# Four conv-like layers on one core: where an output product, a tile copy and the parameter load stand in their queues

## The chip, the cores and the metric

The kernel runs on one core of a Trainium2 chip. The metric is device time in microseconds (us) of the whole program, from the first to the last instruction; the median of several executions counts. A core has a matrix engine (TensorE, PE in the profile; its weight loads are PEld), a vector engine (VectorE, DVE), an activation engine (ScalarE, ACT), GpSimd (POOL) and a queue engine (SyncE, SP) that here only starts DMA transfers. Each engine works through its own instruction list; semaphores order them against each other. PSUM is the accumulator memory that TensorE writes.

## The reference, cut to what matters

Four images of 512 channels and 64 x 64 points go through four layers. Layer 0 is softmax attention over all 4096 points with 64 channels, layer 1 a convolution whose weights are mixed from eight experts by a router, layer 2 a linear attention, layer 3 two discounted running sums with a gate.

```python
# layer 0
t = einsum('oc,bchw->bohw', w_qkv, x)               # key, query, value: 64 channels each
scores = einsum('bdk,bdq->bkq', key_, query)         # 4096 x 4096 for each image
attn = softmax(scores, axis=1)                       # over the keys
out = einsum('bdk,bkq->bdq', value, attn)
x = scale * einsum('oc,bchw->bohw', w_out, out) + x
# layer 1
pooled = x.mean(axis=(2, 3)); rw = sigmoid(pooled @ router_w.T + router_b)
# ... three convolutions with W = sum over experts of rw * experts, batch norms g, b, m, v, relu
# layer 2
Q = softplus(Wq x + bq); K = softplus(Wk x + bk); V = Wv x + bv
KV = einsum('bmn,bcn->bmc', K, V)
x = x + gamma * einsum('bnm,bmc,bn->bcn', Q, KV, 1 / einsum('bnm,bm->bn', Q, K.sum(-1) + EPS))
# layer 3
# ... x + gamma * x_gate * sigmoid(discounted sums of x_scan along both axes)
```

## The kernel before

Everything is in float32. An image's points are worked on in four "pairs" of 2 x 512 points. Double PSUM banks come from one pool of three, which scores, output products and transposes share in turn; there are two single banks beside it.

```python
def pair_psum(name):
    return ps.tile([P, 2, NB], F32, tag="s", name=name, bufs=3)
def bank(name, shape=(P, NB)):
    return ps.tile(list(shape), F32, tag="acc", name=name)   # 2 buffers
```

The kernel starts with loads. `prm` holds all small parameters, 50 floats for each of 128 partitions; the first image's x comes in 16 pieces.

```python
for queue, k in ((nc.scalar, 0), (nc.sync, 2)):
    queue.dma_start(wqkv_sb[:, k:k + 2, :], wqkv_t[:, k:k + 2, :])
prm_sb = const.tile([P, NPRM], F32, tag="prm", name="prm_sb")
nc.scalar.dma_start(prm_sb, prm)
xs = [load_pair(0, pr) for pr in range(NPAIR)]     # b == 0: four pieces of 512 KB for each pair
# ... [cut]
for j, n, _, _, _, v in groups:                     # batch norm from the parameters
    nc.vector.tensor_scalar(bn_v[:, j:j + n], col(v, n), 1e-5, None, ALU.add)          # L155
nc.scalar.activation(bn_s, bn_v, AF.Sqrt)                                               # L156
nc.vector.reciprocal(bn_v, bn_s)                                                        # L157
# ... [cut: three products or differences for each group, L159 to L161]
```

The projections of the first image follow the steps of a list. A digit is a matrix product, `v0:1` a value product of pair 0 with channel piece 1, `seed` a copy by ScalarE (L317) that the product `2` accumulates upon, `t5` the difference of the two pairs (L257) that the product `5` reads.

```python
first = ("zero v0:0 1:0 v0:1 1:1 seed v0:2 2:0 v0:3 2:1 t5 5 c11 v1:0 v1:1 t6 ...")     # [cut]
```

In the attention, a step i computes scores of 128 keys with one pair of queries, their exponential goes to a ring of 12 buffers, VectorE adds it to the pair's sum, and later a product with the values reads it. A pair has 32 steps, a round 8 steps; an image has 16 rounds, numbered 0 to 15. Values lag scores, so a pair ends in rounds 4, 8 and 12, and the last one after the loop.

```python
def scores(i):
    pr, kt = divmod(i, NT)
    s = pair_psum(f"s_{b}_{i}")
    for h in range(2):
        nc.tensor.matmul(s[:, h, :], key[...], qry[...], start=True, stop=True)         # L376
    nc.scalar.activation(p, s, AF.Exp)                                                  # L379
    nc.vector.tensor_tensor(accs[pr], accs[pr], p, ALU.add)                             # L384

def inverse_sums(pr):
    den = bank(f"den_{b}_{pr}")
    # ... [cut] sum over partitions by a product with ones                              # L407
    nc.vector.reciprocal(recs[pr], den)                                                 # L410

def sums(pr, early=True):
    if early:
        inverse_sums(pr)
    # ... [cut] o = av * rec                                                            # L419, L421
    if early:
        sum_range(pr)                              # two reductions of rec, L428, L429

def out_step(pr, m):
    y = pair_psum(f"y_{b}_{pr}_{m}")               # output product                     # L435
    # ... [cut] xs = y * scale + xs, with its sum to pool_acc                           # L440

for g in range(NPAIR * NT // ROUND):
    for i in range(g * ROUND, (g + 1) * ROUND):
        scores(i)
    # ... [cut]
    ended = None
    while done < (g + 1) * ROUND - (RING - ROUND):
        if done == NPAIR * NT - 5:
            inverse_sums(NPAIR - 1)
        pr = values(done)                          # L391
        done += 1
        if pr is not None:
            ended = pr
            if pr < NPAIR - 2:
                late += [(g + 1, lambda pr=pr, m=m: out_step(pr, m)) for m in range(KC)]
    # ... [cut]
    if ended is not None:
        sums(ended)
    if late and late[0][0] <= g:
        late.pop(0)[1]()
# then: pooled sums and router base from pool_acc, L486 to L493
```

In the linear attention, x is transposed in tiles of 128 points (`move`): eight transposes to a double bank, one copy to memory, and a product with the keys reads the copy. Between them stands the softplus of the keys of pairs 2 and 3.

```python
def move(pr, j):
    xtr = pair_psum(f"xtr_{b}_{pr}_{j}")
    # ... [cut] eight transposes                                                        # L738
    xt = four(f"xt_{b}_{pr}_{j}")
    (nc.scalar.copy if j % 2 or (pr > 1 and j) else nc.vector.tensor_copy)(xt, xtr)     # L740
    moved.append(xt)

def products(pr, between=()):
    for j0 in range(0, TPB, 2):
        for step in [lambda j=j: move(pr, j) for j in (2, 3)] if j0 == 0 else between:
            step()
        # ... [cut] products of tiles j0 and j0 + 1                                     # L753

with tc.manual_schedule(engines={mybir.EngineType.DVE}):     # VectorE keeps the program's order
    # ... [cut]
    keys = features(1, (2, 3))
    rest()
    keys = keys()            # ScalarE: Abs, Relu, Exp; VectorE: u = e + 1 (L691); ScalarE: Ln
    products(0, ahead(1))
    keys()
    products(1, ahead(2))
```

Of the kernel before, what the change touches and what calls it, by code (L numbers as in the profile page):

```python
# [24 lines left out]
NPAIR = NBLK // 2  # L25
# [21 lines left out]
def unshifted(ctx: ExitStack, tc: tile.TileContext, fits, x, wqkv_t, wout_t, router_t,  # L47
# [3 lines left out]
    nc = tc.nc  # L51
# [34 lines left out]
    def load_pair(b, pr):  # L86
        if b and pr == NPAIR - 1:
            places[NPAIR - 1:] = places[NPAIR], places[NPAIR - 1]
        t = places[pr]
        src = x[b, :, pr * 2 * NB:(pr + 1) * 2 * NB].rearrange("(kc p) n -> p kc n", p=P)  # L90
        if b == 0:
            for kc in range(KC):
                nc.sync.dma_start(t[:, kc, :], src[:, kc, :])
        else:
            nc.sync.dma_start(t, src)
        return t
# [4 lines left out]
    for queue, k in ((nc.scalar, 0), (nc.sync, 2)):  # L101
        queue.dma_start(wqkv_sb[:, k:k + 2, :], wqkv_t[:, k:k + 2, :])
    prm_sb = const.tile([P, NPRM], F32, tag="prm", name="prm_sb")
    nc.scalar.dma_start(prm_sb, prm)
    def col(i, n=1):
        return prm_sb[:, i:i + n]

    xs = [load_pair(0, pr) for pr in range(NPAIR)]

    a11, a12, a21, a22 = (wqkv_sb[:, k:k + 2, w * D:(w + 1) * D] for w in range(2) for k in (0, 2))  # L110
    wout_sb = const.tile([P, C], F32, tag="wout", name="wout_sb")
# [237 lines left out]
    def layer0(b, xs, pro):  # L349
# [21 lines left out]
# [4 lines that stand above are left out]
                r = slice(h * D, (h + 1) * D)  # L375
                nc.tensor.matmul(s[:, h, :], key[r, kt * P:(kt + 1) * P],  # L376
                                 qry[r, pr * NB:(pr + 1) * NB], start=True, stop=True)
            p = ring[i % RING]
            nc.scalar.activation(p, s, AF.Exp)  # L379
            if kt == 1:  # L380
                accs[pr] = four(f"acc_{b}_{pr}")
                nc.vector.tensor_tensor(accs[pr], ring[(i - 1) % RING], p, ALU.add)
            elif kt > 1:
                nc.vector.tensor_tensor(accs[pr], accs[pr], p, ALU.add)  # L384

        def values(i):
            pr, kt = divmod(i, NT)
            if kt == 0:
                avs[pr] = bank(f"av_{b}_{pr}")
            for h in range(2):  # L390
                nc.tensor.matmul(avs[pr][h * D:(h + 1) * D, :], vt[:, kt, :], ring[i % RING][:, h, :],  # L391
                                 start=kt == 0, stop=kt == NT - 1)
            if kt < NT - 1:
                return None
            if pr < NPAIR - 1:
                av = block(f"avsb_{b}_{pr}")
                nc.scalar.copy(av, avs[pr])
                avs[pr] = av
            return pr
# [3 lines left out]
        def inverse_sums(pr):  # L403
            acc = accs[pr]
            den = bank(f"den_{b}_{pr}")
            for h in range(2):
                nc.tensor.matmul(den[h * D:(h + 1) * D, :], ones[:, 0:D], acc[:, h, :],  # L407
                                 start=True, stop=True)
            recs[pr] = block(f"rec_{b}_{pr}")
            nc.vector.reciprocal(recs[pr], den)  # L410
# [33 lines left out]
        def out_step(pr, m):  # L444
            add_out(pr, m, out_product(pr, m))
# [5 lines left out]
        def pool(pr, kc):  # L451
            xm = xs[pr][:, kc, :]
            nc.scalar.activation(xm, xm, AF.Copy, accum_out=pool_acc[:, kc, pr:pr + 1])

        late, done = [], 0
        with tc.manual_schedule(engines={mybir.EngineType.Activation}):
# [3 lines that stand above are left out]
                if 1 < g < 2 + 2 * KC:  # L460
                    pool(NPAIR - 2 + (g - 2) // KC, (g - 2) % KC)
                if g == 1:
                    pro.key_copies()
# [10 lines that stand above are left out]
                if b == 0 and g == 1:  # L474
                    router = router_of_values()
                if b == 0 and g == 2:
                    router()
                if ended is not None:
                    sums(ended)
                if late and late[0][0] <= g:  # L480
                    late.pop(0)[1]()
        assert not late

# [13 lines left out]
        pr = NPAIR - 1  # L497
# [165 lines left out]
    def layer2(b, xs, sums_of_six, mix_last, conv2, conv3, wcq, qs):  # L663

        ks = small.tile([P, NPAIR], F32, tag="ks", name=f"ks_{b}")
        g = None
# [66 lines left out]
# [3 lines that stand above are left out]
                n0 = h * NB + j * P  # L736
                for kc in range(KC):
                    nc.tensor.transpose(xtr[:, h, kc * P:(kc + 1) * P], xs[pr][:, kc, n0:n0 + P], ident)  # L738
# [3 lines that stand above are left out]

        def products(pr, between=()):
            for j0 in range(0, TPB, 2):
                for step in [lambda j=j: move(pr, j) for j in (2, 3)] if j0 == 0 else between:
                    step()
                for j in range(j0, j0 + 2):
                    t = pr * TPB + j  # L750
                    xt = moved.pop(0)
                    for h in range(2):
                        nc.tensor.matmul(g[h * D:(h + 1) * D, :], kts[pr][:, j, h * D:(h + 1) * D], xt[:, h, :],  # L753
                                         start=t == 0, stop=t == NPAIR * TPB - 1)

        def ahead(pr):
            return [lambda j=j: move(pr, j) for j in range(2)]
# [37 lines left out]
        with tc.manual_schedule(engines={mybir.EngineType.DVE}):  # L795
            key_transpose((0, 1))
            rest = rest()
            move(0, 0)
            move_by_halves(0, 1)
            conv3(3, h2[3])  # L800
            g = bank(f"g_{b}", (P, C))
            keys = features(1, (2, 3))
            rest()
            keys = keys()
            products(0, ahead(1))
            keys()
            products(1, ahead(2))
            kfold = bank(f"kfold_{b}", (P, NPAIR))
            nc.tensor.matmul(kfold, fold, ks, start=True, stop=True)
            ksum = small.tile([P, 1], F32, tag="ksum", name=f"ksum_{b}")  # L810
            nc.vector.tensor_reduce(ksum, kfold, AX.X, ALU.add)
            for h in range(2):
                r = slice(h * D, (h + 1) * D)
                nc.vector.tensor_scalar(kbd[r, 16 * h:16 * (h + 1)], ones[r, 0:16], ksum[r, :], 1e-6, ALU.mult, ALU.add)
            key_transpose((2, 3))
            inv = invert((0, 1))
            products(2, ahead(3))
            divide((0, 1), inv)
            weights[2]()
            products(3)  # L820
            g_sb = block(f"gsb_{b}", (P, C))
            nc.scalar.copy(g_sb, g)
            gt = block(f"gt_{b}", (P, KC, P))

            late = (0, (2, 3), pair_psum(f"z_{b}_0_2"))
            feature_part(*late, 0, 0, 2)

            gk = pair_psum(f"gk_{b}")
            for kc in range(KC):
                nc.tensor.matmul(gk[:, 0, kc * P:(kc + 1) * P], g_sb[:, kc * P:(kc + 1) * P], fold,  # L830
                                 start=True, stop=True)
            nc.scalar.copy(gt, gk[:, 0, :].rearrange("p (kc c) -> p kc c", c=P))
            feature_part(*late, 0, 2, 2)
            kv = small.tile([P, C], F32, tag="kv", name=f"kv_{b}", bufs=1)
            for i in range(2):
                part = slice(i * C // 2, (i + 1) * C // 2)
                kvp = bank(f"kvp_{b}_{i}", (P, C // 2))
                for kc in range(KC):
                    nc.tensor.matmul(kvp, gt[:, kc, :], wv_sb[:, kc, part], start=kc == 0, stop=kc == KC - 1)
                nc.vector.scalar_tensor_tensor(kv[:, part], bv_sb[:, part], ksum, kvp, ALU.mult, ALU.add)  # L840
# [295 lines left out]
    with tc.manual_schedule(engines={mybir.EngineType.PE}):  # L1136
        pro = Projections(0)
        for b in range(B):
# [3 lines left out]
            xs, pro = layer3(b, xs, *layer2(b, xs, *convs))  # L1142
# [442 lines left out]
```

## Time and profile before

| what | before |
|---|---|
| time, median of 3 | 2655.01 us (2654.95 to 2657.95) |
| span of the profiled execution | 2653.7 us |
| TensorE busy | 2636.2 us, 99% |
| VectorE busy | 2017.9 us, 76% |
| ScalarE busy | 1316.2 us, 50% |
| mean granted TensorE clock | 0.999 |

A line of the timeline gives start, duration, engine, source line, operation, the tiles written and read, shapes and count; the brackets at its end give the time that the engine idled before and what ended it. Matmuls are pipelined, and their ends in the profile are modelled. Of the costliest groups, the three of the attention loop are these (line, engine, names, count, busy us, mean ns, idle before):

```profile
L376 PE MATMUL s<-qv,key 64*128 64x512 f32 x2048 | 458.0, 594 | 5.3 <-DVE x L440 3.2
L379 ACT ACTIVATE ring<-s 128x1024 f32<-128x1024 f32 x336 | 317.2, 1050 | 260.3 <-PE s L376 260.3
L384 DVE TENSOR_TENSOR acc<-acc,ring 128x1024 f32<-128x1024 f32 x312 | 382.2, 1225 | 63.2 <-ACT ring L379 35.6
```

### The profile page before, as it was taken

What the parts mean: (1) busy time and instruction counts of PE and PEld (TensorE: products, weight loads), DVE (VectorE), ACT (ScalarE), POOL (GpSimd) and SP (SyncE); (2) the same over time, 40 slices, a digit from 0 to 9 for tenths busy, and PEclk for the clock granted to TensorE, in tenths of its full rate; (3) what the DMA queues carried; (4) which work ended last, traced back from release to release, by engine and by line L of the source; (5) the groups of instructions that cost most, each with busy time, mean ns of one, the idle gap of its engine ahead of it and who ended that gap; (6) DMA issues with size and microseconds to landing.
All of it is one profiled execution on the core that took longest, in us unless ns stands there. A gap on an engine that the chain in (4) does not pass through costs nothing.

```text
span 2653.7 us, 25809 instructions
## 1 busy us (share of the span) xinstructions
PE 2636.2 (99%) x10050; PEld 1116.5 (42%) x10050; DVE 2017.9 (76%) x2272; ACT 1316.2 (50%) x1510; POOL 12.1 (0%) x26
## 2 busy tenths in 40 slices
PE   9999999999999999999999999999999999999998
PEld 3333464344333345444433334544443333554443
DVE  7777866888777786688877778668887777856887
ACT  4554353454555436345556553535555555263545
POOL 1000000000000000000000000000000000000000
PEclk9999999999999999999999999999999999999999
DMA  5000210022200021012220002101121000210001
GB/s 193 1 1 1 103 32 1 27 101 80 80 1 1 1 103 32 1 47 80 80 80 1 1 1 103 32 1 63 64 87 72 0 1 8 97 32 1 32 40 57
DMA packets 34739, 115.17 MB, mean 43 GB/s; under 512 B 3120, under 2 KB 12080, under 8 KB 33072
## 3 DMA queue, kind: packets, MB, share of 16 engines
q1 hardware_dynamic: 34320, 113.21, 11.3%
q8 instruction: 81, 1.33, 0.2%
q14 instruction: 50, 0.41, 0.1%
q10 hardware_dynamic: 288, 0.22, 0.0%
HBM read 79.86 MB, written 33.55 MB: 43 GB/s over the span
## 4 chain that ended last, share of the span: by engine, by line
PE 96%; DVE 2%; ACT 1%; issue 0%; DMA 0%; SPq 0%; ACTq 0%
PE av L391 17%; PE sx L934 16%; PE s L376 16%; PE zy L934 12%; PE z L675 4%; PE c L650 4%; PE c L578 4%; PE c L627 3%; PE wv L852 2%; PE y L435 2%; PE kq L312 2%; PE vv L265 2%; PE g L753 2%; PE xtr L738 2%; PE c2e L627 2%; PE kqz L312 1%
## 5 line engine op out<-in xcount | busy, mean ns | idle before, releaser
L376 PE MATMUL s<-qv,key 64*128 64x512 f32 x2048 | 458.0, 594 | 5.3 <-DVE x L440 3.2
L379 ACT ACTIVATE ring<-s 128x1024 f32<-128x1024 f32 x336 | 317.2, 1050 | 260.3 <-PE s L376 260.3
L384 DVE TENSOR_TENSOR acc<-acc,ring 128x1024 f32<-128x1024 f32 x312 | 382.2, 1225 | 63.2 <-ACT ring L379 35.6
L376 PEld LDWEIGHTS s<-qv,key 64*128 64x128 f32 x2048 | 192.1, 186 | 264.0 <-issue 118.1
L391 PE MATMUL av<-ring,qv 128*64 128x512 f32 x1344 | 302.2, 595 | 0.0
L934 PE MATMUL sx<-t,x 128*128 128x512 f32 x512 | 232.4, 593 | 0.0
L384 DVE TENSOR_TENSOR acc<-acc,x 128x1024 f32<-128x1024 f32 x168 | 205.6, 1224 | 34.7 <-ACT x L379 19.4
L379 ACT ACTIVATE x<-s 128x1024 f32<-128x1024 f32 x176 | 166.7, 1053 | 124.4 <-PE s L376 124.4
L391 PEld LDWEIGHTS av<-ring,qv 128*64 128x64 f32 x1344 | 92.6, 137 | 200.1 <-issue 200.1
L939 ACT COPY zy<-sx 128x512 f32<-128x512 f32 x64 | 36.5, 570 | 253.9 <-PE sx L934 253.9
L391 PE MATMUL av<-x,qv 128*64 128x512 f32 x704 | 159.5, 595 | 0.0
L984 DVE TENSOR_TENSOR_SCAN t<-x,t 128x512 f32<-128x512 f32 x128 | 149.2, 1209 | 1.6
L934 PEld LDWEIGHTS sx<-t,x 128*128 128x128 f32 x512 | 96.7, 190 | 124.6 <-issue 120.9
L943 ACT ACTIVATE e<-sx,prm_sb 128x512 f32<-128x512 f32 x128 | 87.8, 686 | 122.4 <-PE sx L934 122.4
L967 DVE TENSOR_TENSOR_SCAN s<-wc,s 128x512 f32<-128x512 f32 x128 | 146.1, 1202 | 0.0
L973 ACT COPY t<-s 128x1024 f32<-128x1024 f32 x64 | 127.5, 1992 | 29.3 <-DVE s L967 28.7
L990 ACT ACTIVATE s<-t 128x1024 f32<-128x1024 f32 x64 | 125.7, 1990 | 11.2 <-DVE t L984 11.1
L934 PE MATMUL zy<-t,wq 128*128 128x512 f32 x256 | 118.5, 602 | 0.0
L934 PE MATMUL zy<-x,wq 128*128 128x512 f32 x256 | 118.0, 600 | 0.0
L934 PE MATMUL sx<-x,wq 128*128 128x512 f32 x256 | 117.1, 595 | 0.0
L934 PE MATMUL sx<-t,wq 128*128 128x512 f32 x256 | 116.6, 595 | 0.0
L934 PE MATMUL zy<-x,x 128*128 128x512 f32 x256 | 116.3, 594 | 0.0
(227 smaller groups left out, 3451.9 us busy)
## 6 DMA issues: line engine op xcount, KB each, us to landing
out_dram<-s SPq DMA_DIRECT2D x62, 512.0 KB, 2.6
x<-in_x_dram SPq DMA_DIRECT2D x12, 2048.0 KB, 8.4
x<-in_x_dram SPq DMA_DIRECT2D x16, 512.0 KB, 9.7
ex<-in_packed_dram SPq DMA_DIRECT2D x4, 2048.0 KB, 7.7
ex<-in_experts_dram SPq DMA_DIRECT2D x4, 2048.0 KB, 7.9
wq<-in_wproj_t_dram SPq DMA_DIRECT2D x32, 256.0 KB, 5.0
ex<-in_packed_dram SPq DMA_DIRECT2D x4, 1536.0 KB, 6.0
ex<-in_experts_dram SPq DMA_DIRECT2D x4, 1536.0 KB, 6.4
```

Of the source, the lines that this page charges most:

```text
L376: nc.tensor.matmul(s[:, h, :], key[r, kt * P:(kt + 1) * P], qry[r, pr * NB:(pr + 1) * NB], start=True, stop=True)
L379: nc.scalar.activation(p, s, AF.Exp)
L384: nc.vector.tensor_tensor(accs[pr], accs[pr], p, ALU.add)
L391: nc.tensor.matmul(avs[pr][h * D:(h + 1) * D, :], vt[:, kt, :], ring[i % RING][:, h, :], start=kt == 0, stop=kt == NT - 1)
L578: nc.tensor.matmul(y[:, h, :], wc[:, kc, :], xs[pr][:, kc, h * NB:(h + 1) * NB], start=kc == 0, stop=kc == KC - 1)
L627: nc.tensor.matmul(y[:, lo - a:hi - a], u, v[:, lo:hi], start=dy == 1, stop=dy == 2)
L650: nc.tensor.matmul(y[:, h, :], wc[:, KC + 9 + m, :], h2[:, h, :], start=True, stop=True)
L934: nc.tensor.matmul(y, w[:, c, self.kind, self.j * P:(self.j + 1) * P], v[:, c, :], start=c == 0 and k in (1, 5), stop=c == 1, skip_group_c ...
L967: nc.vector.tensor_tensor_scan(self.half(i, h), along[:, self.j + 2 * i, :], self.half(i, h), 0.0, ALU.mult, ALU.add)
L973: nc.scalar.copy(self.t[i].rearrange("p (w r) -> p w r", w=W), self.s[i].rearrange("p (r w) -> p w r", w=W))
L984: nc.vector.tensor_tensor_scan(th, down[:, i, :], th, 0.0, ALU.mult, ALU.add)
L990: nc.scalar.activation(self.s[i].rearrange("p (r w) -> p w r", w=W), tw, AF.Sigmoid)
```

## The change

Three things move; the computation is the same.

1. A round of the attention in which a pair ends does its inversion and leaves a waiting output product to the next round. It is for rounds in which both come together, so that the product's addition does not stand behind the inversion's reciprocal.
2. The third transposed tile of pair 0 is copied before the softplus of the keys of pairs 2 and 3 rather than after its first part. It is for the double bank of that tile to come free sooner.
3. The parameters are loaded on the same queue as x, behind its first pair, rather than on ScalarE's queue beside it. It is for the first pieces of x.

```diff
     prm_sb = const.tile([P, NPRM], F32, tag="prm", name="prm_sb")
-    nc.scalar.dma_start(prm_sb, prm)
     def col(i, n=1):
         return prm_sb[:, i:i + n]
 
-    xs = [load_pair(0, pr) for pr in range(NPAIR)]
+    xs = [load_pair(0, 0)]
+    nc.sync.dma_start(prm_sb, prm)
+    xs += [load_pair(0, pr) for pr in range(1, NPAIR)]
# ... [cut]
                 if ended is not None:
                     sums(ended)
-                if late and late[0][0] <= g:
+                elif late and late[0][0] <= g:
                     late.pop(0)[1]()
# ... [cut]
-        def products(pr, between=()):
+        def products(pr, between=(), more=(2, 3)):
             for j0 in range(0, TPB, 2):
-                for step in [lambda j=j: move(pr, j) for j in (2, 3)] if j0 == 0 else between:
+                for step in [lambda j=j: move(pr, j) for j in more] if j0 == 0 else between:
                     step()
# ... [cut]
             keys = features(1, (2, 3))
             rest()
+            move(0, 2)
             keys = keys()
-            products(0, ahead(1))
+            products(0, ahead(1), (3,))
             keys()
             products(1, ahead(2))
```

## The prediction

> **What bounds the kernel now.** I read the page first. TensorE is busy for all but 17.5 us of the span, so nothing that another engine saves shows unless TensorE waited for it.
>
> ```profile
> PE 2636.2 (99%) x10050; PEld 1116.5 (42%) x10050; DVE 2017.9 (76%) x2272; ACT 1316.2 (50%) x1510; POOL 12.1 (0%) x26
> ```
>
> The second view was the list of what TensorE waited for (releaser, total us, times, longest us). It is the whole list, and it names the three places that the change touches: scores held by the addition of an output product (L440), a transpose held by a copy (L740), the first x piece.
>
> ```profile
> PE s L376 <- DVE x L440: 3.2, 8, 0.4
> PE s L376 <- ACT ring L379: 2.1, 8, 0.3
> PE kqz L305 <- POOL ident masks.py:199: 1.5, 1, 1.5
> PE xtr L738 <- DVE xt L740: 1.0, 4, 0.2
> PE vv L265 <- DMA x<-in_x_dram: 0.8, 1, 0.8
> ```
>
> These totals are too small. A matmul is shown with some 0.59 us although matmuls start closer together than that, so a wait only shows as idle once the modelled end is passed. I therefore took lost time from starts. Third view: the timeline around round 8 of image 0 (start us, us, engine, line), where both an inversion and an output product stand.
>
> ```profile
> 175.71 1.13 PE L435 MATMUL y<-o,wout_sb 64*128 64x512 f32 x4
> 176.68 1.88 PE L376 MATMUL s<-qv,key 64*128 64x512 f32 x8
> 178.82 1.13 PE L376 MATMUL s<-qv,key 64*128 64x512 f32 x4 [0.27 <-ACT ring L379]
> 180.35 4.56 PE L376 MATMUL s<-qv,key 64*128 64x512 f32 x20 [0.40 <-DVE x L440]
> 184.84 1.51 PE L391 MATMUL av<-ring,qv 128*64 128x512 f32 x6
> ...
> 175.83 3.36 DVE L410 RECIPROCAL rec<-den 128x512 f32<-128x512 f32 x1 [2.71 <-PE den L407]
> 179.10 1.18 DVE L440 SCALAR_TENSOR_TENSOR x<-y,prm_sb,x 128x1024 f32<-128x1024 f32 x1
> ```
>
> The product y takes one of the three double PSUM banks at 175.71, and its addition stands behind a 3.36 us reciprocal, so that bank is back at 180.2 only. Meanwhile the scores have two banks: they wait for ScalarE at 178.82 and for y's bank at 180.35. From first score to first value product it is 184.84 - 176.68 = 8.16 us. Round 9, with a product alone, has them at 192.82 and 199.79: 6.97 us. Loss: 1.19 us. Round 4, with an inversion alone, goes from 115.90 to 122.97, 7.07 us, without a wait; its extra 0.1 us is the first score after another row layout, which a round with y pays at y instead.
>
> Fourth view: the timeline at the end of image 0's attention.
>
> ```profile
> 270.02 5.21 DVE L384 TENSOR_TENSOR acc<-acc,ring 128x1024 f32<-128x1024 f32 x4 [3.55 <-ACT ring L379]
> 275.33 5.21 DVE L384 TENSOR_TENSOR acc<-acc,x 128x1024 f32<-128x1024 f32 x4
> 280.91 1.03 PE L407 MATMUL den<-acc,ones 128*64 128x512 f32 x4
> ```
>
> The last sum ends at 275.33 + 5.21 = 280.54, the product that reads it starts at 280.91: 0.37 us to spare, no more.
>
> Fifth view: the same for the move of the linear attention, and for the start of the kernel.
>
> ```profile
> 412.20 1.09 PE L738 MATMUL xtr<-ident,x 128*128 128x128 f32 x8
> 413.53 1.09 PE L738 MATMUL xtr<-ident,x 128*128 128x128 f32 x8 [0.24 <-DVE xt L740]
> ...
> 411.64 0.69 DVE L691 TENSOR_SCALAR sp<-sp 128x1024 f32<-128x1024 f32 x1 [5.24 <-ACT sp L690]
> 412.25 2.35 DVE L740 COPY xt<-xtr 128x1024 f32<-128x1024 f32 x2
> ```
>
> ```profile
> 7.55 0.23 PEld L265 LDWEIGHTS vv<-x,wqkv_sb 128*64 128x64 f32 x4 [0.63 <-DMA x<-in_x_dram]
> 9.55 0.57 ACT L317 COPY kqz<-kq 128x512 f32<-128x512 f32 x1 [3.09 <-PE kq L312]
> 11.45 2.43 DVE L257 TENSOR_TENSOR ring<-x,x 128x1024 f32<-128x1024 f32 x2 [2.69 <-DMA x<-in_x_dram]
> 12.80 2.21 PE L312 MATMUL kqz<-ring,wqkv_sb 128*64 128x512 f32 x8
> ```
>
> VectorE idles 5.24 us before L691 although the transpose that L740 copies was complete at 409.5: only the order of its queue holds the copy back.
>
> **What the Trainium skill says.** "PSUM — Partial Sum Buffer", section "Engine vs sequencer instructions": VectorE and ScalarE queues are strict FIFO, and matmuls start and complete in program order. The trace agrees: the addition of y starts at 179.10, as the 3.36 us reciprocal ends, and 5.24 us go by ahead of L691 with a copy ready behind it. "DMA: Bandwidth & Descriptors", section "Queues, rings and completion order": each DMA engine goes round the queues it has work for, and takes each queue's descriptors in order. So the parameters on ScalarE's queue share the engines with the first piece of x, and behind x on SyncE's queue they cannot. The trace fits: the first two pieces of x land 7.55 - 5.83 = 1.72 us apart, the next three (11.45 - 7.55)/3 = 1.30 us. I read the difference, 0.42 us, as the parameters' share. Same page, "Specifications": transfers want 512 B or more; a parameter row is 50 floats, 200 B, which fits a share so large for 25 KB.
>
> **Part 1, attention rounds.** No instruction is added or removed. With "elif", the product due in round 8 goes to 9, those of pair 1 to rounds 10, 11, 13 and 14; 13 to 15 had none. Removed: 1.19 us in rounds 8 and 12, of four images: 8 x 1.19 = 9.5 us. A product costs TensorE the same wherever it stands. Round 5, a product after an inversion, has one pair of scores 0.04 us late; rounds 9 and 13 now look like it: 8 x 0.04 = 0.3 us back. Net -9.2 us.
>
> Added: the last product is now at the head of the last round. In the built program its addition and then the pooled sums and router base (one reduction and six small operations, which stood between sums in rounds 12 and 13) stand ahead of the last eight sums. Reckoned from the product's start Y, as in round 9 (Y = 191.86): the addition and its accumulator read end at Y + 2.47, the first exponential lets sums begin at Y + 3.09. The small operations take, by their spacing around 245 to 251, 0.19 + 0.19 + 0.19 + 3 x 0.26 + 0.14, some 1.4 us, so sums begin at Y + 3.85, and end 10.52 us later (270.02 to 280.54), at Y + 14.37. TensorE comes to the inversion at 0.96 (192.82 - 191.86) + 6.97 + 6.06 (280.91 - 274.85) = Y + 13.99. It must wait some 0.4 us, in each image: +1.7 us. Part 1 sums to -7.5 us.
>
> **Part 2, the copy first.** TensorE's order is the same; only copy and L691 change places on VectorE. The copy can run from 409.5 to 410.8, before L691's input is there at 411.6, so L691 is not delayed. The transpose at 413.53 would start at 413.13, by eight starts 0.11 us apart after 412.20. -0.4 us, four images: -1.6 us. What follows has room for it: the next reader of a ScalarE copy needs it at 415.0, and it is done at 414.3.
>
> **Part 3, parameters behind x.** The four pieces of pair 0 land 0.42 us sooner, the fourth at 11.45 - 1.30 - 0.42 = 9.7; the parameters at about 10.15; the fifth at 11.45 as before, as the bytes ahead of it are the same. But the batch norm's root stands ahead of the seed copy (9.55) in ScalarE's queue, and needs them: 10.15 + 0.33 (three VectorE operations, 5.93 to 6.26) + 0.21 (root) + 0.57 (copy) puts the seed's end at 11.3 instead of 10.12. And the norm's reciprocal and products, 6.54 to 7.40, 0.86 us, which stood in idle time, now stand between the two differences of L257. The second difference ends 0.86 us later, at 14.75, and the second half of the product shown at 12.80 starts then instead of at 13.93; the seed's own path (1.15 us late at 10.18, three products more) makes it 14.8 too. From there on TensorE has no wait in the start, so this goes to the end: +0.9 us, with the sooner first piece gained and lost again on the way.
>
> **Sum.** -7.5 - 1.6 + 0.9 = -8.2 us: 2655.0 - 8.2 = 2646.8 us.
>
> **The rivals.** (a) The wait moves: with the products in rounds 13 and 14 VectorE falls so far behind in the last round that the inversion waits a microsecond or more per image. For it: 0.37 us to spare. Against: VectorE idles 3.55 us before the last round, and a round costs it 9.8 + 1.4 us of some 15. Time: 2650 to 2653. (b) Nothing is lost at the end (the router's small operations overlap the wait for the first exponential better than reckoned) and the parameters land in time for the seed, so that the start gains 0.4 us instead of losing 0.9: 2655.0 - 9.2 - 1.6 - 0.4 = 2643.8. (c) The list of waits is literal: only 3.2 + 1.0 us go, with the ScalarE wait staying, 2651. Against it: round 4, with an inversion alone, has no wait for ScalarE.
>
> **Range and chances.** The steps with the least ground are the last round (0 to 3 us) and the start (-0.4 to +1.6). They give 2643.8 to 2649; with the 3 us between the three times before I take 2643.0 to 2651.0. 2% is 53 us, three times all of TensorE's idle time, so faster by that is out of reach, and nothing added is near it.
>
> **What would show it.** Right: no wait of scores for L440 or ScalarE; rounds 8 and 12 at 7.07 us from score to value product; a new wait of the fourth inversion (L407) for L384 in all images; the second half of the seeded product near 14.8 us; no wait for L740. Wrong: a wait for L440 in rounds 13 or 14, an inversion held over 1 us, or a seed copy that ends near 9.7 us.

## The result, and the profile after

The changed kernel takes 2648.48 us (2647.67 to 2648.85), the kernel before beside it 2654.82 us (2653.98 to 2657.95): a ratio of 0.9974, 95% interval 0.9962 to 0.9987. It is faster by 0.26%, within 2%, and 1.7 us slower than predicted. Lines of its code are numbered one higher than before where the prediction names them (L376 is now L377).

Busy time by engine, from the page: TensorE was busy for 2636.2 us and is for 2632.7 us, with as many instructions.

```profile
PE 2632.7 (99%) x10050; PEld 1116.7 (42%) x10050; DVE 2019.7 (76%) x2272; ACT 1314.3 (50%) x1510; POOL 12.2 (0%) x26
```

What TensorE waits for in the changed kernel (releaser, total us, times, longest us), the whole list:

```profile
PE den L408 <- DVE acc L385: 2.2, 4, 0.5
PE kqz L306 <- POOL ident masks.py:199: 1.5, 1, 1.5
PE kqz L313 <- ACT kqz L318: 1.3, 1, 1.3
PE vv L266 <- DMA x<-in_x_dram: 0.4, 1, 0.4
```

Three entries are gone: scores for the addition, scores for ScalarE, transposes for the copy. Two are new: the fourth inversion of each image for its sums, and a product for the seed copy. But a list of waits doesn't say how much each costs. So I cut both traces at the first instruction of each stage of TensorE:

| stage (us from start to start) | before | after | difference |
|---|---|---|---|
| start of the span to the first scores | 46.47 | 47.60 | +1.13 |
| attention, first image | 241.61 | 240.07 | -1.54 |
| attention, each later image | 240.04 | 238.49 | -1.55 |
| convolutions and linear attention, first three images | 135.87 | 135.41 to 135.42 | -0.46 |
| the same, last image | 136.19 | 135.99 | -0.20 |
| span of this execution | 2653.7 | 2646.8 | -6.9 |

The attention gives 6.2 us, the stage of the copies 1.6 us, and the start takes 1.1 us; together -6.7 of the -6.9.

The timeline of TensorE at round 8 of image 0 (start us, us, engine, line), now with an inversion and no product. As in the prediction, the scores that follow a round's inversion or product are counted to that round; by the code they are the first work of the next.

```profile
176.85 7.14 PE L377 MATMUL s<-qv,key 64*128 64x512 f32 x32
183.92 7.09 PE L392 MATMUL av<-ring,qv 128*64 128x512 f32 x32
```

From the first score to the first value product it is 183.92 - 176.85 = 7.07 us, 8.16 before. The scores are one unbroken group of 32, where before two waits cut them into three.

The last round of image 0's attention, VectorE first and then TensorE:

```profile
268.26 0.17 DVE L487 TENSOR_REDUCE pooled<-pool 128x4 f32<-128x16 f32 x1
...
269.87 5.21 DVE L385 TENSOR_TENSOR acc<-acc,ring 128x1024 f32<-128x1024 f32 x4
275.18 5.21 DVE L385 TENSOR_TENSOR acc<-acc,x 128x1024 f32<-128x1024 f32 x4
...
265.76 1.13 PE L436 MATMUL y<-o,wout_sb 64*128 64x512 f32 x4
...
280.45 1.08 PE L408 MATMUL den<-acc,ones 128*64 128x512 f32 x4 [0.54 <-DVE acc L385]
```

The product starts at Y = 265.76. The pooled sums and router base hold VectorE from 268.26 to 269.87, the eight sums then to 275.18 + 5.21 = 280.39, and the inversion follows at 280.45. The idle time that is listed is 0.54 us; from the last value product's start to the inversion's it is 1.13 us in place of 0.42 before, so the loss is 0.71 us, and the second half of the inversion's product comes 0.05 us later still (0.47 us behind the first, not 0.42).

VectorE around the copy of the linear attention:

```profile
409.15 1.23 DVE L741 COPY xt<-xtr 128x1024 f32<-128x1024 f32 x1 [3.16 <-PE xtr L739]
411.24 0.69 DVE L692 TENSOR_SCALAR sp<-sp 128x1024 f32<-128x1024 f32 x1 [0.86 <-ACT sp L691]
```

The copy fills a part of the idle time ahead of L692, which isn't later for it: 0.86 us of idle time remain.

The start of the kernel (ScalarE, VectorE, TensorE):

```profile
10.94 0.58 ACT L318 COPY kqz<-kq 128x512 f32<-128x512 f32 x1
...
13.79 1.22 DVE L258 TENSOR_TENSOR ring<-x,x 128x1024 f32<-128x1024 f32 x1
...
11.57 1.08 PE L313 MATMUL kqz<-x,wqkv_sb 128*64 128x512 f32 x4 [1.29 <-ACT kqz L318]
...
14.20 1.94 PE L313 MATMUL kqz<-ring,wqkv_sb 128*64 128x512 f32 x8
```

The seed copy now ends at 11.52, behind the batch norm's root, and TensorE waits for it. The norm's reciprocal and products (12.93 to 13.8) lie between the two differences, the second of which ends at 13.79 + 1.22 = 15.01.

### The profile page after: what moved, and what is told of

The parts are those of the page before. It is cut to its first block, busy times and chain, and to the rows that moved or that the text cites. A ratio compares the mean times of both kernels' runs of the same rounds, so it can differ in the third digit from the quotient of the medians.

```text
span 2646.8 us, 25800 instructions
## 1 busy us (share of the span) xinstructions
PE 2632.7 (99%) x10050; PEld 1116.7 (42%) x10050; DVE 2019.7 (76%) x2272; ACT 1314.3 (50%) x1510; POOL 12.2 (0%) x26
## 3 DMA queue, kind: packets, MB, share of 16 engines
q8 instruction: 81, 1.33, 0.2%
## 4 chain that ended last, share of the span: by engine, by line
PE 96%; DVE 2%; ACT 1%; DMA 0%; issue 0%; SPq 0%; DVEq 0%; ACTq 0%
PE sx L936 16%; PE av L392 16%; PE s L377 16%; PE zy L936 12%; PE z L676 4%; PE c L651 4%; PE c L579 4%; PE c L628 3%; PE wv L854 3%; PE y L436 2%; PE g L754 2%; PE xtr L739 2%; PE kq L313 2%; PE vv L266 2%; PE kqz L313 2%; PE c2e L628 2%
## 5 line engine op out<-in xcount | busy, mean ns | idle before, releaser
L377 PE MATMUL s<-qv,key 64*128 64x512 f32 x2048 | 454.1, 593 | 0.0
L377 PEld LDWEIGHTS s<-qv,key 64*128 64x128 f32 x2048 | 192.7, 186 | 254.1 <-issue 112.4
L992 ACT ACTIVATE s<-t 128x1024 f32<-128x1024 f32 x64 | 125.7, 1990 | 11.3 <-DVE t L986 11.1
```

The costliest lines, as they stand in the source:

```text
L377: nc.tensor.matmul(s[:, h, :], key[r, kt * P:(kt + 1) * P], qry[r, pr * NB:(pr + 1) * NB], start=True, stop=True)
L992: nc.scalar.activation(self.s[i].rearrange("p (r w) -> p w r", w=W), tw, AF.Sigmoid)
```

## The experiments

Theory: 1.19 us were lost in each round with both, as y's bank stands behind the reciprocal; most of it is gained, but some is lost again at the fourth inversion, which the router's small operations hold up; the start loses a microsecond through the order of two queues. The rivals are those of the prediction. Each time is a median beside runs of the kernel before on the same chip, each ratio with its 95% interval.

**One part at a time.** First the rounds alone, in the kernel before:

```diff
-                if late and late[0][0] <= g:
+                elif late and late[0][0] <= g:
```

> Only part 1 of the change (the output product leaves rounds with an inversion). Theory from starts: 8 rounds lose 1.19 us less, 0.3 us comes back in rounds 9 and 13, and the fourth inversion waits 0.7 us per image: -9.5 + 0.35 + 2.8 = -6.3 us, so 2648.5 us against 2654.8, with the wait of L407 for L384 in all four images. Rival, the list of waits read literally (3.2 + 2.1 us of idle, then the new wait of 2.2 us): -3.1 us, 2651.7 us.

Measured: 2648.38 us, ratio 0.9976 (0.9967 to 0.9986). The attention takes 240.04 and then 238.46 us, 1.58 less in each image. The waits for the addition and for ScalarE are both gone, though the list gave them 5.3 us in all for a loss of 9.5; the wait for the copy stays at 1.0 us; the inversion has its new wait (2.1 us in four). The reading from starts holds, the literal one falls.

Then the copy alone, and the parameters alone:

```diff
+            move(0, 2)
             keys = keys()
-            products(0, ahead(1))
+            products(0, ahead(1), (3,))
```

> Only part 2 (the third tile's copy ahead of the softplus). Theory from starts: -0.40 us per image, -1.6 us, 2653.2 us, the wait of L738 for L740 gone. Rival, list of waits literal: -1.0 us. Second rival, that the copy's earlier memory tile delays the softplus on ScalarE: 0 or slower.

Measured: 2653.22 us, ratio 0.9994 (0.9986 to 1.0003). The interval holds 1, so the time doesn't settle it. The trace does: convolutions and linear attention take 135.41 us in place of 135.87 in each of the first three images, 135.73 in place of 136.19 in the last, and no transpose waits for L740.

```diff
-    nc.scalar.dma_start(prm_sb, prm)
-    xs = [load_pair(0, pr) for pr in range(NPAIR)]
+    xs = [load_pair(0, 0)]
+    nc.sync.dma_start(prm_sb, prm)
+    xs += [load_pair(0, pr) for pr in range(1, NPAIR)]
```

> Only part 3 (parameters on SyncE's queue behind x's first pair). Theory: the first piece of x comes 0.25 us sooner, but the seed copy waits for the batch norm's root: the scores start 1.1 us later, 2655.9 us. Rival, what the change is for: 0.25 us sooner at the first product is 0.25 us sooner at the end, 2654.6 us.

Measured: 2655.88 us, ratio 1.0004 (0.9996 to 1.0012), again not settled by the time. In the trace the first scores come at 47.44, with a wait of 0.5 us for the seed copy, which starts as the root has run.

**Is it the order behind the reciprocal that costs a round with both?** The kernel before keeps both in a round, but the product goes first:

```diff
-                if ended is not None:
-                    sums(ended)
                 if late and late[0][0] <= g:
                     late.pop(0)[1]()
+                if ended is not None:
+                    sums(ended)
```

> Before, with the two statements of a round exchanged: the waiting output product stands ahead of the inversion, in the same round, so its addition stands ahead of the reciprocal. Theory (the loss is the PSUM bank held behind the reciprocal, not the amount of work in the round): no wait for L440 in rounds 8 and 12; two more changes of row layout of 0.1 us each stand against 1.19 us, and the last round stays as it was: 8 x 1.0 = -8.0 us, 2646.8 us. Rival (a round has too much for VectorE with both): the wait stays or moves to the ring, 2652 to 2655 us.

Measured: 2649.18 us, ratio 0.9979 (0.997 to 0.9987). The timeline of round 8 (VectorE, then TensorE):

```profile
175.85 1.28 DVE L440 SCALAR_TENSOR_TENSOR x<-y,prm_sb,x 128x1024 f32<-128x1024 f32 x1 [2.91 <-PE y L435]
177.06 3.35 DVE L410 RECIPROCAL rec<-den 128x512 f32<-128x512 f32 x1
...
176.74 7.14 PE L376 MATMUL s<-qv,key 64*128 64x512 f32 x32
```

With the addition ahead of the reciprocal the 32 scores run through, in a round that still has both: it is the order, not the amount of work in that round. The gain is 1.48 us an image, less than expected. y now stands between two products of another tile shape (value product 128\*64, y 64\*128, inversion 128\*64, scores 64\*128: three changes where there was one). From the value products ahead of y and the inversion to the next value products it is 183.81 - 167.66 = 16.15 us, and 184.84 - 167.84 = 17.00 us before. The run told of below that puts the reciprocal last has the inversion first and no wait there, and takes 183.71 - 167.91 = 15.80 us: the two changes more cost 0.35 us. Round 9 loses another 0.23 us (7.20 us in place of 6.97), as its addition starts 1.47 us behind y, 1.18 us before. Twice 0.85 less 0.23 is the 1.48 us but for 0.01.

**Does the start's loss come from where the norm stands?** In the changed kernel the norm's operations become a step of the list behind `t5`, so that ScalarE has the seed copy and VectorE both differences ahead of them:

```diff
-    for j, n, _, _, _, v in groups: ...      # [cut] the norm, ahead of the list
+    def norms(): ...                         # [cut] the same operations
-    first = ("... 2:1 t5 5 c11 ...")
+    first = ("... 2:1 t5 norm 5 c11 ...")
```

> The changed kernel with the batch norm's operations behind the seed copy and behind the first differences (t5); the parameters stay behind x's first pair. Theory (the start loses because the seed copy and the second difference stand behind the parameters): the seed copy ends near 10.2 us, the second half of the product upon it starts near 14.3 us instead of 15.1, -0.8 us against the changed kernel, 2647.6 us; the scores start 0.3 us later than before the change, as the fifth piece of x came 0.3 us later. Rival (the transfer order itself costs the start): scores start where they did, 2648.4 us.

Measured: 2647.51 us, ratio 0.9973 (0.9963 to 0.9984). The first scores are at 46.55, 1.05 us sooner than in the changed kernel. ScalarE and TensorE in this run:

```profile
9.95 0.57 ACT L319 COPY kqz<-kq 128x512 f32<-128x512 f32 x1 [7.49 <-PE kq L312]
...
13.20 1.89 PE L312 MATMUL kqz<-ring,wqkv_sb 128*64 128x512 f32 x8
```

The seed copy ends 1.00 us sooner (10.52), nothing waits for it, and the product on the differences starts at 13.20 and runs through; its second half starts at 14.06. The rival, that the order of the transfers costs the microsecond, falls. The two paths were not parted by a run: in the changed kernel the second difference ends at 15.01, and the late seed alone brings TensorE to the second half at 15.06 too. ScalarE pays for it with a second table load of 1.28 us, in idle time.

**Does the router's chain hold the inversion?** In the changed kernel the pooled sums and the base go behind the last sums. VectorE's instructions, which a scheduler orders in this loop, are kept in the program's order for that:

```diff
-        with tc.manual_schedule(engines={mybir.EngineType.Activation}):
+        with tc.manual_schedule(engines={mybir.EngineType.DVE, mybir.EngineType.Activation}):
                     if done == NPAIR * NT - 5:
+                        pooled_base()        # the seven operations from L487 to L494
                         inverse_sums(NPAIR - 1)
```

> The changed kernel with VectorE in program order in the attention loop, and the pooled sums and router base behind the last eight sums instead of ahead of them. Theory (the new wait of the fourth inversion is the 1.6 us of small operations ahead of the last sums): the wait of L407's product is gone, 0.7 us per image, -2.8 us against the changed kernel, 2645.7 us. Rival (the last round waits because the addition of the last output product itself came into it): at least half of the wait stays, 2647 us or more.

Measured: 2650.91 us, ratio 0.9985 (0.9979 to 0.9992), a gain of 3.7 us where the changed kernel gains 6.3. The wait of the inversion is gone, but the scores have a new wait for the addition, 3.5 us in 12. VectorE at the reciprocal of round 4 shows why:

```profile
116.27 3.36 DVE L411 RECIPROCAL rec<-den 128x512 f32<-128x512 f32 x1 [2.71 <-PE den L408]
119.73 0.69 DVE L422 TENSOR_TENSOR o<-avsb,rec 128x512 f32<-128x512 f32 x1
```

o needs the reciprocal and stands directly behind it; in the changed kernel the scheduler had put a sum between. The next addition, in round 5, is then 15.70 us behind the reciprocal's start (131.97), 15.25 us in the changed kernel (117.15 to 132.40). Of the 0.45 us, 0.19 are o's later start (119.73 - 116.27 = 3.46 us behind the reciprocal's, against 3.27 us for the sum); the rest is that o, behind a sum, starts 1.08 us after it, and a sum behind a sum 1.33 us. A pair of scores there, and in rounds 9 and 13, starts 0.82 us or more behind the one before, not 0.425, and such a round takes 7.46 us in place of 7.01: 12 x 0.45 = 5.4 us lost, against the 3.1 us that the inversions no longer wait. I had changed two things with one edit, so I did it again. On top of the edit above, only the chain now moves against the changed kernel; o and the reductions wait, as they did there, until a sum of the next round is done:

```diff
                     scores(i)
+                    if ended is not None:
+                        sums(ended)          # o and the reductions, no inversion
+                        ended = None
...
                 if ended is not None:
-                    sums(ended)
+                    inverse_sums(ended)
```

> The changed kernel with nothing moved but the pooled sums and router base, behind the last eight sums; VectorE's order in the other rounds is that of the changed kernel, with one sum between reciprocal and output, which e5 had not. Theory: the wait of the fourth inversion is gone (0.7 us per image, -2.8 us) and no wait for the addition of a product comes, so 2645.7 us. If the wait is gone and the time is not, the 0.7 us per image come back at the reciprocal or the router behind it, 2648 us.

Measured: 2645.59 us, ratio 0.9963 (0.995 to 0.9977). The last round, VectorE and TensorE:

```profile
278.92 0.16 DVE L458 TENSOR_REDUCE pooled<-pool 128x4 f32<-128x16 f32 x1
...
265.38 1.13 PE L434 MATMUL y<-o,wout_sb 64*128 64x512 f32 x4
...
279.37 1.03 PE L408 MATMUL den<-acc,ones 128*64 128x512 f32 x4
```

The sums begin at 268.48, Y + 3.10, the chain runs behind them, and the inversion starts at 279.37 - 265.38 = Y + 13.99 without a wait. The chain ahead of the sums was the whole of that wait. Three images gain 0.77 us or more by it. The second gains 0.42 only: VectorE idles 0.46 us, not 0.10, between two sums of its round 9 (at 846.54), the addition comes late, and the round takes 7.36 us in place of 7.01. So VectorE has no room to spare in the round behind a reciprocal.

**Everything mended at once.** On top of the first run on the chain, the one that was slower, the parameters go behind x's second pair and the norm behind `t4`:

```diff
-    xs = [load_pair(0, 0)]
+    xs = [load_pair(0, pr) for pr in range(2)]
     nc.sync.dma_start(prm_sb, prm)
-    "v2:0 v2:1 t4 7 e3 ..."
+    "v2:0 v2:1 t4 norm 7 e3 ..."
```

> Parts 1 and 2 with the router base behind the last sums, the parameters behind x's second pair, and the batch norm behind the differences t4. Theory: -9.15 us (rounds, no new wait), -1.6 us (copy), -0.4 us (all of x's first eight pieces sooner, nothing waits for the parameters): 2643.8 us against 2654.9. Rival: VectorE or ScalarE pay for the later batch norm (a second table load on ScalarE) and the start stays as before or gets slower, 2644.2 us or more.

Measured: 2649.3 us, ratio 0.998 (0.9972 to 0.9988). It has the same order behind the reciprocal, and the same wait for the addition (2.8 us in 12).

**Could a round keep both, with the reciprocal last?** As the last run, but with the `if` of the kernel before, and in a round with both first the inversion's product, then y and its addition, then the reciprocal (the chain of the pooled sums stands behind the loop again):

```diff
+            if between is not None:
+                between()                    # out_step: y and its addition
             recs[pr] = block(f"rec_{b}_{pr}")
             # ... [cut] the reciprocal
```

> As e7, but part 1 in another way: a round keeps both, TensorE's order is that of before (inversion's product, then output product), and only the reciprocal stands behind the addition on VectorE. Theory (what counts is the bank behind the reciprocal): no wait for L440 in rounds 8 and 12, no new layout change, some 0.23 us lost in round 9 as in e4, so -8.6 - 1.6 - 0.4: 2644.3 us. Rival (one of two banks back too late, as the addition now waits for the output product): waits of L376 for L440 stay in part, 2646 us or more.

Measured: 2652.58 us, ratio 0.9993 (0.9984 to 1.0001). Round 8 is as fast as any (176.75 to 183.71), but round 9 isn't. VectorE's next addition, and TensorE's scores there:

```profile
193.86 1.28 DVE L444 SCALAR_TENSOR_TENSOR x<-y,prm_sb,x 128x1024 f32<-128x1024 f32 x1
...
195.20 4.99 PE L378 MATMUL s<-qv,key 64*128 64x512 f32 x22 [1.63 <-DVE x L444]
```

The next product's addition stands behind the reciprocal and eight sums, and its bank comes back so late that scores wait 1.63 us. From the reciprocal's start (178.17) it is 15.69 us, as in the first chain run (15.70), of which 0.45 us are the program's order; the rest of the delay is that the reciprocal itself starts 1.21 us later, behind the addition at 176.96. The attention takes 239.97 us an image, 240.04 before: the loss has only moved by a round. With the product first, above, the reciprocal starts 1.11 us sooner than here, since y stands ahead of the inversion, and round 9 loses only 0.23 us. So it does matter how much VectorE has to do, over two rounds.

**The version that beats both.** As the second run on the chain, with the two reductions of the reciprocal put behind the next round's addition, and parameters and norm as in the run with everything mended:

```diff
-            if early:
-                sum_range(pr)                # two reductions in the round of o
                     late.pop(0)[1]()
+                if stats is not None:
+                    sum_range(stats)         # now behind the next addition
```

> Parts 1 and 2, the router base behind the last sums, one sum between reciprocal and output, the two reductions of the reciprocal put off behind the addition of the next round, the parameters behind x's second pair and the batch norm behind the differences t4. Theory: -9.5 us (rounds, none of it given back), -1.6 us (copy), -0.35 us (start): 2643.2 us against 2654.7. Rival: VectorE's put-off reductions hold up a later addition or ring buffer, 2645 us or more.

Measured: 2643.28 us (2642.47 to 2643.82), ratio 0.9955 (0.9941 to 0.9968). Its attention takes 239.15 us and then 237.58, 2.46 less than before. TensorE still waits for the first constant (1.5 us) and the first x (0.4 us), and for nothing else.

The start's share isn't shown. The first scores of single profiles lie at 46.03 to 46.47 with the start unchanged (four profiles, mean 46.27), at 46.73 to 47.60 with the parameters behind the first pair and the norm ahead (four, mean 47.25), and at 45.99 to 46.75 with both mended (three, mean 46.28). The loss of a microsecond is clear in the means, though the groups touch (46.73 and 46.75); a gain of 0.4 us is not.

## Why the prediction was right, and where a size was off

*The loss from starts, 8 x 1.19 us.* Right. Rounds 8 and 12 take 7.07 us, and the rounds alone bring 1.58 us an image although the list of waits gave only 5.3 us in all. The cause named, y's bank behind the reciprocal, is shown by the run with the product first.

*0.04 us back in rounds 9 and 13.* Right: one pair of scores in each starts 472 to 485 ns behind the one before, in place of 425.

*The fourth inversion waits 0.4 us.* The wait is there, in every image, for the cause named, and moving the chain removes it; the term was too small. Y + 13.99 for TensorE's arrival was exact, as the second run on the chain shows. The small operations were taken as 1.38 us (2.47 to 3.85). Already the terms written down sum to 1.49, and the spacing in the trace, where the first of the three operations counted at 0.26 took 0.18, to 1.41. That was their cost between sums; one behind the other they take 269.87 - 268.26 = 1.61 us, and start at Y + 2.50 rather than 2.47. The sums therefore end at Y + 14.63 and not at Y + 14.37, and the inversion starts 0.06 us after that, at Y + 14.69. That is 0.70 us, and 0.05 more with the second half of its product: four times 0.75 is 3.0 in place of 1.7 us. So an image gains -2 x 1.19 + 2 x 0.05 + 0.75 = -1.53 by these terms, and -1.55 by the stages; part 1 is -6.2 rather than -7.5 us.

*The copy, 4 x 0.4 us.* Right: 0.46 in each image with the copy alone; in the changed kernel 0.46 in three images and 0.20 in the last, together 1.6. (The copy was ready for the last 2.1 of VectorE's 5.24 us of idle time, from 409.5 to 411.64, not for all of them.) The last image lacks 0.25 us against the copy's run. All four profiles with the parameters behind the first pair and the norm ahead of the seed show these 0.25 us, that of the parameters alone too (136.44 for 136.19), so they belong to part 3 and not to the copy. They arise where ScalarE idles 0.36 us behind a small function of the router (L519); in the last image of the other eight it idles 0.08 us there. Why is open.

*The start, +0.9 us.* Right in sign, path and nearly in size. Seed copy done at 11.52 (11.3 predicted), second difference at 15.01 (14.75), second half of the product at 15.06 (14.8); the first scores are 1.13 us later in this pair of profiles, 1.0 in the means. The fifth piece of x was expected at 11.45 as before, but its difference starts at 11.79. The first piece gained nothing that can be told from the scatter: TensorE's first product is 0.24 us sooner in the changed kernel (5.62) and later with the parameters alone (6.39). And the reading behind it, that the parameters' share of the engines held x back by 0.42 us, was wrong. The run with the copy alone has the old order of loads, and there the second piece's weights are loaded 7.06 - 5.71 = 1.35 us after the first piece's, not 1.72:

```profile
5.71 0.23 PEld L265 LDWEIGHTS vv<-x,wqkv_sb 128*64 128x64 f32 x4 [2.05 <-issue]
...
7.06 0.17 PEld L265 LDWEIGHTS vv<-x,wqkv_sb 128*64 128x64 f32 x2 [0.26 <-DMA x<-in_x_dram]
```

By the landings in the traces, the first two pieces are 1.78 us apart in the profile before and 1.24 to 1.32 in the three other runs with the old order: the 0.42 us were the scatter of one execution. What the parameters do take shows where they stand ahead of the fifth piece. It lands 1.37 to 1.40 us behind the fourth in the five runs with the parameters there, and 1.27 to 1.29 in the other seven: some 0.1 us. The prediction gained and lost its 0.42 us again within its sum, so the mistake did not reach the total.

*The rivals.* (a), a wait of a microsecond or more at the inversion, is wrong in size but close in kind: 0.7 us. That VectorE's backlog can eat the gain is true of other orders, as the reciprocal put last and the program order showed. (b), nothing lost at the end and the start sooner, was not the changed kernel; 2643.28 us shows that about as much could be had. (c), the literal list, falls with the rounds alone.

*The sum.* Predicted -8.2 us. By the stages of one pair of profiles it is -6.2 - 1.6 + 1.1 = -6.7, by the medians -6.3: 1.3 us are missing in part 1, all in the one term of the fourth inversion, and 0.2 in the start; the other 0.4 is within what single executions differ by (2647.67 to 2648.85).

## What to carry to other kernels

Take lost time from the starts of a saturated engine's instructions, not from its list of waits. What gives a shared bank back should not stand behind a long instruction of an in-order queue; before moving it, follow that queue through the next round and the last one, where the loss may return. A load that is moved also delays all that stands behind its first reader in two queues, so move that reader with it.

## What was not expected of the hardware

- A VectorE instruction that needs the result of the one ahead of it starts later than one that doesn't: 3.46 us after the reciprocal's start (o, 116.27 to 119.73) against 3.27 us (a sum, 117.15 to 120.42). Sums that add to the same tile start 1.33 us apart (four from 121.53 to 126.83), o behind a sum 1.08 us after it (120.42 to 121.50). Seven small operations in a chain show the same, 1.61 us in place of 1.41. The Trainium skill, "VectorE: DVE Perf Modes", section "The DRAIN you can't avoid", reports that in a row of eight copies a semaphore behind each cost nothing extra; for these dependent pairs the trace has 0.19 to 0.25 us. Whether it is the semaphore that takes them isn't shown.
- Now and then VectorE idles 0.46 us between two sums of the attention, in place of 0.10, at least once in each of the twelve profiles. Most of these pauses cost nothing. One in the round behind a reciprocal cost 0.35 us (7.36 for 7.01 us, in the second image of two runs). The cause is open.
- Changing between tile shapes 128\*64 and 64\*128 on TensorE costs 0.1 to 0.2 us each time: the first pair of scores behind another shape takes 0.53 us in place of 0.425, and two changes more made the same work 0.35 us longer in the run with the product first. "TensorEngine Tiling (Array Packing)", section "Key Properties", says that a change of tiling mode, not just of the tile, drains TensorE. The trace fits that; it can't tell a drain from another cause.
- A wait can cost far more than its listed idle time: 5.3 us listed for 9.5 lost, 1.0 for 1.8 (the copy, 4 x 0.46), 0.54 for 0.71.
